# A one-core graph-attention layer: five more tiles add two products on VectorE, seven lists instead of eight beside the k|v rows, second half of the feed-forward weights asked later, x gathers pinned in their queue

## The chip, the cores and the metric

The kernel runs on 1 core of one Trainium2 chip. The metric is the device time of one execution in microseconds. A core has five engines with a queue each: TensorE (PE, its weight loads shown as PEld), VectorE (DVE), ScalarE (ACT), GpSimd (POOL) and SyncE (SP). Each works through its own queue in order. DMAs are started from the queues of SP, ACT and POOL; the indirect ones (gathers and scatters by row number) all come from POOL.

## The reference

One layer of masked attention over 4096 nodes with a feed-forward block, all in float32. `adj` holds about 17 edges in a row, so the work is sparse.

```python
hs = layer_norm(x, ln1_scale, ln1_bias); ht = layer_norm(h_target, ln1_scale, ln1_bias)
q = (ht @ Wq + bq).reshape(T, H, HD) / sqrt(HD)          # T = S = 4096, H = 8, HD = 64
k = (hs @ Wk + bk).reshape(S, H, HD)
v = (hs @ Wv + bv).reshape(S, H, HD)
logits = where(adj != 0, einsum('thd,shd->hts', q, k), -1e30)
probs = softmax(logits, axis=-1)
ctx = einsum('hts,shd->thd', probs, v).reshape(T, D)      # D = 512
ht = layer_norm(ht + ctx @ Wo + bo, ln2_scale, ln2_bias)
ff = gelu(ht @ W1) @ W2                                   # W1 512 x 2048, W2 2048 x 512
out = layernorm(x + ht + ff)
```

## The kernel before, in words

**First stage, to about 275 us.** Two things run side by side. `project` reads x, normalizes it and multiplies with Wk and Wv (L947); ScalarE copies the products (L949) and its queue writes rows of k|v, 1024 floats each, to a table `kvd` in DRAM (L953). `edges` turns a tile of 128 rows of `adj` into lists of neighbours: SP loads quarters of the rows (L714), ScalarE takes the sign and counts (L733), VectorE multiplies by column numbers (L740), finds the largest of segments (L742), and decodes and ranks them (L749 to L766). The 4096 target rows are handled in two parts of 16 tiles. `prepare` makes the lists of the first part and `sort(0)` orders its rows by degree with a scatter (L871). `fill` then makes `FILL = 8` list tiles of the second part while k|v rows are still being made. `RINGED` says how many tiles may load adj into free slots of the ring; later ones use two spare slots.

**Second stage, from about 277 us.** Sorted tiles of 128 targets are worked on in turn; the number of neighbour slots of a tile is its cap. In the order of work, tiles 0 to 15 are the first part with caps 11, 13, 14, 15, 15, 16, 17, 17, 18, 19, 19, 20, 22, 23, 24, 39, and tile 16 (12) begins the second part, with 38, 13, 24, 14, 23, 15 and so on after it. Tiles form groups: tile 0 alone, then pairs, and the last one alone. For a tile, `front` gathers the targets' rows, normalizes them (L1017, behind a small VectorE instruction L1013 that waits for the last k|v row) and makes the query (L1030, L1035). The slots go in segments of S = 3. `issue` gathers three rows of `kvd` per segment on POOL (L985) into a ring of 17 slots in the first part and 20 in the second; `request` keeps AHEAD = 4 segments asked for, five in the second part. VectorE multiplies k by the query (L1241) and sums (L1246), ScalarE takes the exponential (L1250, L1259). `by_scalar` multiplies the third slot's v on ScalarE, eight heads one by one (L1225); `values` multiplies the other two on VectorE (L1202). Each slot's product is then added up over the slots by TensorE as four transposes into PSUM (L1213, 128 x 128 each). In `values`, tiles from NA = 16 on first add slot 1 to slot 0 on VectorE (L1206), so slot 1 needs no transposes; from DENSE = 21 on every other segment also adds the third slot (L1209). `finish` scales by the softmax sum, multiplies by Wo (L1134) and normalizes.

**Feed-forward.** `feed` works one group at a time: `hidden` is W1 and gelu (L1346, L1349) and `output` is W2 (L1355). W1 and W2 come in four quarters of 2 MB each; two are loaded in the first stage, two by `weights` from the ACT queue (L586, L587) at the start of the second. Halfway through a group it gathers the group's x rows (L1373, recorded as L985 with tile xt), and `end` adds them, normalizes and scatters the result (L1323).

**Order.** `_weave` merges the streams by planned cost: every `yield` advances its stream's clock, and the stream that is furthest behind goes next. In the second stage attention and feed-forward take UNIT = 60 units for a pair of tiles; the lists of the second part start at WAIT = 100 units with 12 x 2.2 = 26.4 units a tile, and `sort(1)` follows them with 68 units. This gives the order of tracing. A scheduler then fills each engine's queue, mostly in that order, but an instruction whose inputs and buffers are free early may be put ahead. `with behind(ins)` (an `issue_after`) forbids that: what it holds stays in its engine's queue behind the instruction named. `issues` names the last gather that was traced. `newest` in `weights` names the last by_scalar product, so the ACT queue starts a weight load behind it.

Of the kernel before, what the change touches and what calls it, by code (L numbers as in the profile page):

```python
# [377 lines left out]
DEG, TGT, ROW, RST, E0 = 0, 1, 2, 3, 5  # L378
# [45 lines left out]
def _take(gen, n):  # L424

    for _ in range(n):
        cost = next(gen, StopIteration)
        if cost is StopIteration:
            return
        yield cost  # L430
# [13 lines left out]
def adj_resnorm_kernel(  # L444
# [56 lines left out]
    NA, NBT = len(CAPS_A), len(CAPS_B)  # L501
# [31 lines left out]
    with tc.tile_pool(name="keep", bufs=1) as keep:  # L533
# [13 lines left out]
        tags = keep.tile([P, NT, 2], I32, name="tags")  # L547
# [3 lines left out]
        with ExitStack() as late:  # L551
# [31 lines left out]
            def load_quarter(pool, q, engine=nc.sync):  # L583
                w1.append(pool.tile([P, KC, D], F32, name=f"w1_{q}"))
                w2.append(pool.tile([P, KC, D], F32, name=f"w2_{q}"))
                engine.dma_start(w1[q], W1[:, q * D:(q + 1) * D].rearrange("(c p) n -> p c n", p=P))  # L586
                engine.dma_start(w2[q], W2[q * D:(q + 1) * D, :].rearrange("(c p) n -> p c n", p=P))  # L587
# [115 lines left out]

            adjs = []
            DEEP = 8
            FILL = 8
            RINGED = NA + FILL - 1

            def quarter(i, h):
                if i < RINGED:  # L710
                    a = ring[:, (i * NQ + h) % DEEP, :].bitcast(I32)
                else:
                    a = turn_of("wide", wide)
                nc.sync.dma_start(a, adj[i * P:(i + 1) * P, h * QW:(h + 1) * QW])  # L714
                return a

            def behind(ins):
                return tc.issue_after(ins[-1]) if ins else nullcontext()

            def edges(i):  # L720
# [4 lines left out]
                for h in range(NQ):  # L725
# [9 lines left out]
                    while len(adjs) < min(max(n + 3, min(ahead, RINGED * NQ)), NT * NQ):  # L735
                        adjs.append(quarter(*divmod(len(adjs), NQ)))
                    yield 0.0 if i < NA else 0.7 if i < NA + FILL else 1.0
                    wd = sg.bitcast(U16)
# [6 lines left out]
                    if h % 2 and moms:  # L745
                        moments(moms.pop(0))
                    yield 1.8 if i < NA else 0.7 if i < NA + FILL else 1.0
                dec = dec_w
# [10 lines left out]
                for r in range(RE // 8):  # L759
                    top = rec[:, E0 + r * 8:E0 + (r + 1) * 8]  # L760
                    nc.vector.max(top, flat)
                    if r + 1 < RE // 8:
# [4 lines left out]
                                        op1=ALU.add, accum_out=cnt[:, i:i + 1])  # L767
                yield 2.4 if NA <= i < NA + FILL else 4.0

# [37 lines left out]
            def moments(i):  # L807

                while asked and len(asked) > NT - 4 - i:
                    ask(asked.pop(0))  # L810
                t = hrow(i)
                stats(ip, t, mvh[:, i, :], "n0")
# [169 lines left out]
            issues, logits = [], []  # L982

            def gather(dst, table, idx):
                issues[:] = [nc.gpsimd.indirect_dma_start(  # L985
                    out=dst, out_offset=None, in_=table[:, :],
                    in_offset=bass.IndirectOffsetOnAxis(ap=idx, axis=0)).ins]
# [71 lines left out]
            def request(k):  # L1059


                ahead = AHEAD + (1 if k >= first_b else 0)
                while issued[0] <= min(k + ahead, len(SG) - 1):
# [121 lines left out]
            def attention():  # L1185
# [10 lines left out]
                def values(i, j0, n, kv, p, cps, after):  # L1196

                    m = n - 1 if n == S else n  # L1200
                    v4 = kv[:, :m, D:].rearrange("p j (h d) -> p j h d", h=H)
                    nc.vector.tensor_tensor(v4, v4, p[:, j0:j0 + m, :].unsqueeze(3)  # L1202
                                            .to_broadcast([P, m, H, HD]), ALU.mult)
                    slots = list(range(n))
                    if m > 1 and i >= NA:
                        nc.vector.tensor_add(kv[:, 0, D:], kv[:, 0, D:], kv[:, 1, D:])  # L1206
                        slots.remove(1)
                        if n == S and i >= DENSE and j0 // S % 2:
                            nc.vector.tensor_add(kv[:, 0, D:], kv[:, 0, D:], kv[:, S - 1, D:])  # L1209
                            slots.remove(S - 1)  # L1210
                    for j in slots:
                        for c in range(KC):
                            nc.tensor.matmul(cps[:, c, :], kv[:, j, D + c * P:D + (c + 1) * P], ident,  # L1213
                                             is_transpose=True, start=j0 + j == 0 and c == 0,
                                             stop=j0 + n == TILES[i][1] and j == slots[-1],
                                             skip_group_check=True)
                    if after is not None:
                        tails.append(after)
# [112 lines left out]
            def feed(g):  # L1331
                while g not in h2Ts:
                    yield None
                group, h2T = GROUPS[g], h2Ts.pop(g)
                nt = len(group)
                w = nt * P
                fb = 4 // nt
                cost = UNIT * nt / 2 / (2 * FC // fb)
                xs = []
                po = [psf.tile([P, D], F32, name=f"po{j}", bufs=1) for j in range(nt)]  # L1340

                def hidden(f0):
                    pf = psf.tile([P, fb, w], F32, name="pf")
                    for k in range(fb):
                        for kc in range(KC):
                            nc.tensor.matmul(pf[:, k, :], w1[(f0 + k) // KC][:, kc, (f0 + k) % KC * P:((f0 + k) % KC + 1) * P],  # L1346
                                             h2T[:, kc, :w], start=kc == 0, stop=kc == KC - 1)
                    gt = sp.tile([P, fb, w], F32, name="gt")
                    nc.scalar.activation(gt, pf, AF.Gelu_apprx_tanh)  # L1349
                    return f0, gt  # L1350

                def output(f0, gt):
                    for j in range(nt):
                        for k in range(fb):
                            nc.tensor.matmul(po[j], gt[:, k, j * P:(j + 1) * P], w2[(f0 + k) // KC][:, (f0 + k) % KC, :],  # L1355
                                             start=False, stop=f0 + k == FC - 1, skip_group_check=True)

                def wind_up():
                    for e in list(ends):
                        if next(e, StopIteration) is StopIteration:  # L1360
                            ends.remove(e)

                last = hidden(0)
                wind_up()
                yield cost
                for f0 in range(fb, FC, fb):
                    now = hidden(f0)
                    wind_up()
                    yield cost
                    if f0 == FC // 2:  # L1370
                        for i in group:
                            xt = sp.tile([P, D], F32, name="xt")
                            gather(xt, x, tags[:, i, TGT:TGT + 1])  # L1373
                            xs.append(xt)
                    if f0 == fb:

                        for j in range(nt):
                            for kc in range(KC):
                                nc.tensor.matmul(po[j][:, kc * P:(kc + 1) * P],
                                                 h2T[:, kc, j * P:(j + 1) * P], ident,  # L1380
                                                 is_transpose=True, start=kc == 0, stop=False,
                                                 skip_group_check=True)
                    output(*last)
                    last = now
                    yield cost
                output(*last)
                yield cost
                ends.append(end(group, xs, po))
                if g + 1 == len(GROUPS):
                    while ends:  # L1390
                        wind_up()

                    nc.vector.scalar_tensor_tensor(flag, raised, xs[-1][0:1, 0:1], raised,  # L1393
                                                   op0=ALU.bypass, op1=ALU.max)
# [5 lines left out]

            WAIT = 100.0
            AHEAD = 4
            DENSE = 21
            UNIT = 60.0

# [41 lines left out]
            def fill():  # L1447
# [3 lines left out]
                yield 1.0  # L1451
                for cost in _take(ed, FILL * steps):
                    yield cost
# [9 lines left out]
            def weights():  # L1463


                for q, pool in enumerate(pools):
                    yield 10.0
                    with tc.issue_after(newest[-1]):
                        load_quarter(pool, q + 2, nc.scalar)

# [43 lines left out]
```

## Time and profile before

| | |
|---|---|
| median of 4 runs | 1802.0 us (1793.12 to 1813.67) |
| profiled execution | 1800.15 us, span 1798.4 us |
| mean granted TensorE clock | 0.971 |
| PE busy | 1665.9 us, 93% |
| DVE busy | 1412.2 us, 79% |
| ACT busy | 1223.3 us, 68% |
| POOL busy | 963.1 us, 54% |
| DMA | 461.01 MB, mean 256 GB/s |
| first and last L1206 | 1008.0 and 1656.2 us |
| first L1346, last L1355 | 348.1 and 1775.2 us |

Busy time is the time in which an engine had an instruction running; "idle before" in a list of groups or in brackets of a timeline is the time that the engine stood before that instruction, with what released it. A name such as kv<-kvd,rec is what the instruction writes and reads. The span is one execution's first to last instruction; the small rest up to the profiled execution's time is start and end.

### The profile page before, as it was taken

How to read it: one execution, taken by the hardware profiler on the slowest of the kernel's cores; microseconds unless marked ns; L12 is line 12 of the kernel's file. 1: busy time of each engine (PE TensorE's matmuls, PEld its weight loads, DVE VectorE, ACT ScalarE, POOL GpSimd, SP SyncE). 2: the span in 40 equal slices, each digit the busy share in tenths (PEclk: the TensorE clock that was granted, in tenths of full speed). 3: DMA queues.
4: the chain of work that ended last, by engine and by line, in shares of the span. 5: the costliest groups of instructions: out<-in, count | busy, mean ns of one | idle time of the engine just before them, and what ended most of it. 6: DMA issues, size and time to landing. Idle time of an engine off the chain costs nothing. (4 is left out here: it accounts for less than half of the span.)

```text
span 1798.4 us, 22591 instructions
## 1 busy us (share of the span) xinstructions
PE 1665.9 (93%) x6918; PEld 1082.8 (60%) x6918; DVE 1412.2 (79%) x2432; ACT 1223.3 (68%) x3121; POOL 963.1 (54%) x818
## 2 busy tenths in 40 slices
PE   7999994797999999998998999989999999999995
PEld 3444442665666666666676666655666666666663
DVE  6887787988888779776878999798889888988100
ACT  5876673668677877665767787677878677776210
POOL 1000147745545556787667787867475676671100
PEclk9999997898999999999999999999999999999997
DMA  9999989968878777679778898778686777782000
GB/s 354 381 393 356 349 276 371 340 237 293 268 240 295 234 264 242 226 244 310 251 247 306 284 300 279 237 271 266 205 290 225 268 252 238 238 280 92 24 1 26
DMA packets 142060, 461.01 MB, mean 256 GB/s; under 512 B 18549, under 2 KB 23497, under 8 KB 141929
## 3 DMA queue, kind: packets, MB, share of 16 engines
q0 software_dynamic: 96144, 342.27, 56.2%
q1 hardware_dynamic: 37968, 94.12, 14.8%
q10 hardware_dynamic: 7816, 23.08, 3.3%
q8 instruction: 57, 0.93, 0.2%
q14 instruction: 75, 0.61, 0.1%
HBM read 430.61 MB, written 28.79 MB: 255 GB/s over the span
## 5 line engine op out<-in xcount | busy, mean ns | idle before, releaser
L985 POOL DMA_INDIRECT kv<-kvd,rec x603 | 745.9, 1237 | 329.0 <-PE cps L1213 140.9
L1355 PE MATMUL po<-w,gt 128*128 128x512 f32 x1024 | 465.1, 597 | 5.3 <-ACT gt L1349 5.3
L1346 PE MATMUL pf<-h2T,w 128*128 128x256 f32 (+1 forms) x2176 | 464.4, 367 | 0.3 <-ACT h2T L1165 0.3
L1346 PEld LDWEIGHTS pf<-h2T,w 128*128 128x128 f32 x2176 | 388.0, 190 | 63.6 <-issue 19.6
L1241 DVE TENSOR_TENSOR kv<-kv,tq 128x1536 f32<-128x1536 f32 (+2 forms) x211 | 351.4, 1674 | 77.1 <-DMA kv<-kvd,rec 61.1
L1225 ACT ACTIVATE kv<-kv,pa 128x64 f32<-128x64 f32 x1520 | 391.9, 336 | 4.6
L1246 DVE TENSOR_REDUCE lg<-kv 128x24 f32<-128x1536 f32 (+2 forms) x211 | 350.3, 1666 | 0.7
L1355 PEld LDWEIGHTS po<-w,gt 128*128 128x128 f32 x1024 | 188.8, 192 | 200.9 <-issue 193.6
L1213 PEld LDWEIGHTS cps<-ident,kv 128*128 128x128 f32 x1896 | 225.2, 144 | 98.4 <-issue 42.7
L1213 PE MATMUL cps<-ident,kv 128*128 128x128 f32 x1896 | 250.2, 279 | 33.8 <-DVE kv L1202 26.9
L1202 DVE TENSOR_TENSOR kv<-kv,p 128x1024 f32<-128x1024 f32 (+1 forms) x211 | 250.5, 1191 | 13.9 <-ACT p L1250 13.9
L687 POOL TENSOR_TENSOR n_rs<-n_ve,mhalf 128x2 f32<-128x2 f32 (+2 forms) x51 | 49.2, 964 | 341.6 <-DVE n_ve L680 166.4
L733 ACT ACTIVATE kv<-kv 128x1024 uint8<-128x1024 int32 x128 | 134.4, 1052 | 56.1 <-DMA kv<-in_adj_dram 18.4
L1349 ACT ACTIVATE gt<-pf 128x512 f32<-128x512 f32 x128 | 76.4, 597 | 93.7 <-PE pf L1346 92.6
L1030 PE MATMUL t<-wq,tq 128*128 128x512 f32 x256 | 124.0, 630 | 16.6 <-ACT tq L1024 16.6
L1349 ACT ACT_TABLE_LOAD x104 | 133.4, 1283 | 1.7
L947 PE MATMUL pq<-wv,h2T 128*128 128x512 f32 x256 | 117.1, 601 | 7.1 <-ACT kv L949 4.3
L947 PE MATMUL pq<-wk,h2T 128*128 128x512 f32 x256 | 119.0, 608 | 0.7 <-DMA wk<-in_L_gnn_Wk_dram 0.7
L1134 PE MATMUL t<-wo,rb 128*128 128x512 f32 x256 | 115.5, 593 | 0.0
L1250 ACT ACTIVATE p<-lg 128x24 f32<-128x24 f32 (+2 forms) x179 | 39.0, 218 | 104.0 <-DVE lg L1246 103.0
L742 DVE MAX8 cand<-kv 128x8 uint16<-128x171 uint16 (+1 forms) x384 | 108.1, 324 | 1.2
L1030 PEld LDWEIGHTS t<-wq,tq 128*128 128x128 f32 x256 | 50.2, 202 | 75.5 <-issue 48.4
(163 smaller groups left out, 1561.9 us busy)
## 6 DMA issues: line engine op xcount, KB each, us to landing
kv<-in_adj_dram SPq DMA_DIRECT2D x128, 512.0 KB, 6.8
kvd<-tq ACTq DMA_DIRECT2D x23, 512.0 KB, 6.8
kv<-kvd,rec POOLq DMA_INDIRECT x603, 5.8
kv<-in_L_gnn_h_target_dram SPq DMA_DIRECT2D x32, 256.0 KB, 6.3
kv<-in_x_dram SPq DMA_DIRECT2D x15, 512.0 KB, 7.9
kvd<-kv ACTq DMA_DIRECT2D x9, 512.0 KB, 9.5
w<-in_L_gnn_W_dram SPq DMA_DIRECT2D x4, 1024.0 KB, 7.8
w<-in_L_gnn_W_dram ACTq DMA_DIRECT2D x4, 1024.0 KB, 15.3
```

What stands on the lines that cost most here:

```text
L733: nc.scalar.activation(sg, a, AF.Sign, accum_out=dpart[:, i, h:h + 1])
L947: nc.tensor.matmul(pkv, hT[:, kc, j * P:(j + 1) * P], w[:, kc, :], start=kc == 0, stop=kc == KC - 1)
L985: issues[:] = [nc.gpsimd.indirect_dma_start(out=dst, out_offset=None, in_=table[:, :], in_offset=bass.IndirectOffsetOnAxis(ap=idx, axis=0) ...
L1030: nc.tensor.matmul(pq, hT[:, kc, :], wq[:, kc, :], start=kc == 0, stop=kc == KC - 1)
L1202: nc.vector.tensor_tensor(v4, v4, p[:, j0:j0 + m, :].unsqueeze(3) .to_broadcast([P, m, H, HD]), ALU.mult)
L1213: nc.tensor.matmul(cps[:, c, :], kv[:, j, D + c * P:D + (c + 1) * P], ident, is_transpose=True, start=j0 + j == 0 and c == 0, stop=j0 + n ...
L1225: newest[:] = [nc.scalar.mul(v, v, pa[:, hd:hd + 1]).ins]
L1241: nc.vector.tensor_tensor(kv[:, :n, :D], kv[:, :n, :D], tq[:, :D].unsqueeze(1).to_broadcast([P, n, D]), ALU.mult)
L1246: logits[:] = [nc.vector.tensor_reduce(lg[:, :n, :], kv[:, :n, :D].rearrange("p j (h d) -> p j h d", h=H), AX.X, ALU.add).ins]
L1346: nc.tensor.matmul(pf[:, k, :], w1[(f0 + k) // KC][:, kc, (f0 + k) % KC * P:((f0 + k) % KC + 1) * P], h2T[:, kc, :w], start=kc == 0, stop= ...
L1349: nc.scalar.activation(gt, pf, AF.Gelu_apprx_tanh)
L1355: nc.tensor.matmul(po[j], gt[:, k, j * P:(j + 1) * P], w2[(f0 + k) // KC][:, (f0 + k) % KC, :], start=False, stop=f0 + k == FC - 1, skip_g ...
```

## The change

Four edits. In `values` the limit from which two products are added on VectorE goes from NA = 16 to ADDS = 11, so tiles 11 to 15 add too. FILL goes from 8 to 7, so one list tile moves from the first stage to the lists beside the attention (and RINGED from 23 to 22). The gather of x rows in `feed` is put behind the last gather traced before it. `weights` waits 26 planned units instead of 10 before the third quarter; the fourth then follows at 36 instead of 20.

```diff
-            FILL = 8
+            FILL = 7
             RINGED = NA + FILL - 1
...
-                    if m > 1 and i >= NA:
+                    if m > 1 and i >= ADDS:
                         nc.vector.tensor_add(kv[:, 0, D:], kv[:, 0, D:], kv[:, 1, D:])
                         slots.remove(1)
...
                             xt = sp.tile([P, D], F32, name="xt")
-                            gather(xt, x, tags[:, i, TGT:TGT + 1])
+                            with behind(issues):
+                                gather(xt, x, tags[:, i, TGT:TGT + 1])
                             xs.append(xt)
...
             AHEAD = 4
+            ADDS = 11
             DENSE = 21
...
                 for q, pool in enumerate(pools):
-                    yield 10.0
+                    yield 26.0 if q == 0 else 10.0
                     with tc.issue_after(newest[-1]):
                         load_quarter(pool, q + 2, nc.scalar)
```

## The prediction

> **What bounds the kernel now.** I read the page's busy shares first, then a table of stretches (the first attention tile, the stage of the last five tiles of the first part, a group after it), then the waits of that stage, and last the timeline of the change of stages.
>
> ```profile
> PE 1665.9 (93%) x6918; PEld 1082.8 (60%) x6918; DVE 1412.2 (79%) x2432; ACT 1223.3 (68%) x3121; POOL 963.1 (54%) x818
> ```
>
> TensorE is busy 93% of the span, VectorE 79%. By stretches (columns: stretch in us, its length, then busy time of PE, PEld, DVE, ACT, POOL, the granted clock, DMA share, GB/s):
>
> ```profile
> 288.20:313.10 24.90, 7.14 (x38) 5.28 (x36) 18.15 (x13) 7.34 (x31) 19.86 (x17) 0.76 1.03 403
> 348.10:730.40 382.30, 358.58 (x1668) 247.98 (x1667) 311.96 (x530) 280.55 (x718) 216.60 (x186) 0.97 0.75 258
> 730.40:832.10 101.70, 98.05 (x461) 68.31 (x460) 73.20 (x78) 67.17 (x183) 80.56 (x73) 1.00 0.79 257
> 832.10:927.10 95.00, 89.61 (x434) 63.57 (x433) 80.01 (x86) 68.93 (x199) 58.26 (x51) 1.00 0.78 261
> 927.10:1002.80 75.70, 70.55 (x330) 49.88 (x329) 63.88 (x55) 56.32 (x162) 54.26 (x46) 0.95 0.86 293
> 1028.90:1121.60 92.70, 90.54 (x410) 61.18 (x409) 92.08 (x95) 71.81 (x210) 73.78 (x55) 1.00 0.87 288
> ```
>
> The limits are found from the first L1246 of each tile. 288 to 313 is tile 0: no engine is full, the DMA is. 730 to 832 is tiles 11 and 12 (20 and 22 slots), 832 to 927 tiles 13 and 14 (23 and 24), 927 to 1003 tile 15 (39): these five get the new add. There TensorE is idle 14.2 of 272.4 us and VectorE 55.3. So TensorE sets the pace, with VectorE not far behind. 1029 to 1122 is the group of 38 and 13 slots, which adds already: VectorE is busy 92.08 of 92.7 us (0.993), so it can be loaded to the brim in this loop. After 1672 only feed-forward matmuls are left, 108 us that no edit touches.
>
> **The adds.** A segment is three slots; ScalarE takes the third, VectorE the other two, so each segment with at least two slots left gets one add L1206 and loses the four transposes L1213 of slot 1. The caps 20, 22, 23, 24, 39 make 7 + 7 + 8 + 8 + 13 = 43 adds and 172 transposes fewer.
>
> ```profile
> L1213 PE MATMUL cps<-ident,kv 128*128 128x128 f32 x1896 | 250.2, 279 | 33.8 <-DVE kv L1202 26.9 <-DVE kv L1206 6.7
> L1206 DVE TENSOR_TENSOR kv<-kv 128x512 f32<-128x512 f32 x101 | 68.5, 681 | 0.3
> ```
>
> On VectorE: 43 x 0.681 = 29.3 us more. On TensorE: 250.2/1896 = 0.132 us each by busy time, but the timeline has twelve that start at 380.64 with the next work at 381.95, so 0.109 us from start to start; I take the second, 172 x 0.109 = 18.8 us less (22.7 by the first). What of it reaches the end, group by group:
> - Tiles 11, 12: TensorE 98.05 - 14 x 0.436 = 91.9 busy, VectorE 73.2 + 9.5 = 82.7. TensorE still leads; all 6.1 us come off.
> - Tiles 13, 14: VectorE 80.0 + 16 x 0.681 = 90.9 overtakes TensorE (89.6 - 7.0 = 82.6). The floor is 90.9/0.993 = 91.5 against 95.0: 3.5 us.
> - Tile 15: VectorE 63.9 + 8.9 = 72.8, floor 73.3 against 75.7: 2.4 us.
>
> Sum 12 us. Bounds: 0 if VectorE's waits stay as they are; 18.8 if VectorE's run-ahead lets TensorE keep all.
>
> What can spoil the floor is that VectorE's idle time here is waits, which do not fill by themselves (waits of VectorE from 730 to 1003: total us, times, longest):
>
> ```profile
> DVE kv L1241 <- DMA kv<-kvd,rec: 22.7, 13, 6.4
> DVE tq L1035 <- PE t L1030: 13.4, 2, 8.0
> ```
>
> The first (L1241 behind gathers) shrinks when VectorE comes later to the data, the second when TensorE comes sooner. I therefore let the adds fill them. POOL's gathers are touched as well. In the timeline after 430 us, the 193 kv gathers whose first 0.94 us overlaps no VectorE instruction with two SBUF tensors took 0.95 us on POOL, the 334 that overlap one took 1.41. That is 334 x 0.46 = 154 us on 650 us of such VectorE work, 0.24 per us; the adds make 29.3 x 0.24 = 7 us, and POOL is idle 80 us in this stage. I put it at nothing; if POOL's cover were gone it is 7 us.
>
> The Trainium skill has a rule that speaks against this edit: its page GPSIMD Engine Reference (section 8, Key points) says that GpSimd shares its SBUF interfaces with VectorE and contends with instructions that have two SBUF inputs, which the add is. The rule gives no size; read as the whole 29.3 us lost to POOL it would still fit in the 80 us of POOL's idle time, and the rows' 7 us fits better, so both leave the sum as it is.
>
> **Seven list tiles instead of eight.** One list tile is on VectorE 4 x (0.41 + 3 x 0.324) + 3.2 (the decode and the three rounds of L761/L763) = 8.7 us, on ScalarE 4 x (1.052 + 0.191) = 5.0 us, and 2 MB of adj. It leaves the end of the first stage and joins the lists beside the attention, where it ends in the planner's units at 100 + 9 x 26.4 = 338 instead of 311, and sort(1) with its sixteen POOL scatters L871 at 406 instead of 379, that is in tiles 10 to 13 and not 10 to 12; prefetch of the second part's first records is traced at about 407 and used two tiles later. In its new place TensorE leads (358.6 of 382.3 us busy from 348 to 730) and VectorE has 70 us idle: cost 2 us, bounds 0 and 8.7. POOL's scatters (1.0 us each) are the same number, moved past gathers in a stage with POOL 80 us idle.
>
> **The change of stages** holds the gain of this edit, of the pin and of the later weights (timeline: start, us, engine, line):
>
> ```profile
> 270.85 0.33 ACTq L953 DMA_DIRECT2D kvd<-kv  x1
> 273.73 1.23 POOL L985 DMA_INDIRECT xt<-in_x_dram,tags  x1 [11.98 <-DVE tags L1016]
> 275.09 1.06 ACT L733 ACTIVATE kv<-kv 128x1024 uint8<-128x1024 int32 x1 [1.44 <-DMA kv<-in_adj_dram]
> 276.15 1.50 ACT L1017 ACTIVATE tq<-tq,rec 128x512 f32<-128x512 f32 x2
> 277.06 0.94 POOL L985 DMA_INDIRECT kv<-kvd,rec  x1 [0.85 <-DMA kv<-in_adj_dram]
> 286.43 1.76 DVE L1241 TENSOR_TENSOR kv<-kv,tq 128x1536 f32<-128x1536 f32 x1
> 300.08 0.52 ACTq L587 DMA_DIRECT2D w<-in_L_gnn_W_dram  x1
> 305.32 1.76 DVE L1241 TENSOR_TENSOR kv<-kv,tq 128x1536 f32<-128x1536 f32 x1 [2.24 <-DMA kv<-kvd,rec]
> 311.47 1.76 DVE L1241 TENSOR_TENSOR kv<-kv,tq 128x1536 f32<-128x1536 f32 x1 [4.39 <-DMA kv<-kvd,rec]
> ```
>
> The eighth list tile's signs (L733 at 267.3, 268.4, 272.5, 275.1) stand ahead of the first query's L1017, and its VectorE work ahead of L1013. Without it L1017 runs some 4.6 us sooner. But the first gather needs the last kvd row (written from 270.85), and then 1.24 us per issue and 5.8 us to land: data at 279.56 + 5.8 = 285.4, so only 1.0 of the 4.6 counts, plus up to 3.4 us if signs hold the last k|v copies less (PE waited 3.39 us at 258.8 for L949). I take 2, bounds 0 and 4.6. The two x gathers at 273.73 and 275.28 are the only ones ahead of the attention; pinned behind the last gather traced they leave POOL's queue, 2 x 1.24 = 2.5 us, but the kvd row is the cover: 0, within the same bounds. Later x gathers already stand behind gathers that were traced earlier: 0.
>
> **The weights.** The four 1 MB loads (ACT queue, 290.4 to 300.5) take 4 MB / 403 GB/s = 10.4 us out of a DMA that is full, while gathers come every 1.24 us. VectorE then waits 2.24 + 4.39 = 6.6 us before 313, with TensorE (11.4 us at 304.7 to 316.1) behind it. After the change the first pair goes out at 26 units instead of 10, after the third segment's ScalarE products (about 300 us), the second at 36 instead of 20, in tile 1 (about 315). By then gathers have run ahead: a segment costs 3 x 1.24 = 3.7 us of DMA and 4.6 us of VectorE. A pair delays them 5.2 us, under the four segments (18 us) that are asked ahead. The weights are used from 369 on (third L1346 block), so they have 40 us. Gain 6.6 us; bounds 6.6 and 0 (the hole only moves to tiles 1 and 2, where VectorE is never idle).
>
> **Sum** on the profiled execution, 1800.15 us (span 1798.4 and 1.75 around it): - 12.1 (adds) - 2 (start) - 6.6 (weights) + 2 (list) = -18.7, so 1781.5, say **1782 us**. The profiled time stands 1.85 us under the median 1802.0, inside the runs' 1793 to 1814. About 1% (18 us) is what a measurement of this kernel can tell from no change, so the forecast lies just past that line, below 1784. Its own range, 1773 to 1791, comes from half of each term's bounds.
>
> **Rivals.**
> - The adds turn to nothing (chance 0.16): VectorE's waits for gathers and L1030 stay, and TensorE's freed time becomes waits on L1206. For it: groups after 1122 already show PE waiting for L1206 (6.7 us in all); against: the group at 0.993. 1781.5 + 12.1 = 1794.
> - The weights' hole only moves (0.14): the ring of 17 slots is short, POOL waits for slots already at 317 and 322. Against: the run-ahead above. 1781.5 + 6.6 = 1788.
> - More is won (0.11): from 409.1 to 420.4 TensorE stands 11.29 us behind L1017, which waits for a tq gather that POOL issued late at 411.13. If the new order of POOL's queue issues it in time, 1781.5 - 11.3 = 1770.
> - Slower (0.14): VectorE is on the path all along. In each segment the product, the sum, the new add and the next product are one queue, with four segments ahead and 17 ring slots, not five and 20 as after 1029. Then 29.3 + 8.7 = 38 us are added and 8.6 won at the stages: 1800.15 + 29.4 = 1830. It decides from the point where more than 8.6 of the 38 us are not hidden. Against it: 55.3 us of VectorE idle in the five tiles and 14.2 of TensorE.
>
> **How the numbers follow.** Forecast 0.45, of which 0.34 under 1784; with "more is won" 0.11 that makes faster 0.45. Within 1%: 0.11 + 0.16 + 0.14 + 0.02 of the slow rival = 0.43. Slower 0.12. The range, 1763 to 1812, takes in the first three rivals and the bounds (adds 18.8, start 4.6: 1772; the won stall below that), and leaves out most of the slow one.
>
> **What would show it.** First L1241 near 284 to 285 and no wait on kvd gathers in tile 0; tile 1 from about 305; first L1346 near 340, not 348. The weights' DMAs after 297. 144 L1206 instead of 101, 1724 L1213 instead of 1896. Tiles 11 to 15 in about 260 us instead of 272, VectorE over 90% busy from 832 on. The lists' last L740 some 25 to 40 us later than 683.7. I am wrong if these five tiles take 270 us or more, if tile 1 starts no earlier than 311, or if PE waits for L1206 by more than 15 us before tile 16.

## The result, and the profile after

The changed kernel takes 1797.8 us (median), the kernel before beside it 1798.9 us: ratio 0.9992, 95% interval 0.9982 to 1.0001. No difference can be measured, where 1782 us was forecast. The profiled execution took 1803.2 us (span 1801.4, granted clock 0.962), before 1800.15 us (span 1798.4, 0.971).

The page's busy shares of the changed kernel:

```profile
PE 1661.5 (92%) x6746; PEld 1074.8 (60%) x6746; DVE 1432.7 (80%) x2475; ACT 1230.6 (68%) x3125; POOL 1008.4 (56%) x818
```

The instruction counts are those of the change: 172 matmuls fewer, 43 VectorE instructions more. VectorE is 20.5 us busier, yet TensorE only 4.4 us less busy, though 172 x 0.109 = 18.8 us of work had gone (the last section shows where the rest went), and POOL is 45 us busier with the same 818 instructions. Groups of instructions (busy, mean ns | idle before and what ended it):

```profile
L1213 PE MATMUL cps<-ident,kv 128*128 128x128 f32 x1724 | 240.1, 286 | 66.0 <-DVE kv L1206 39.8 <-DVE kv L1202 25.9
L1206 DVE TENSOR_TENSOR kv<-kv 128x512 f32<-128x512 f32 x144 | 97.8, 680 | 0.3
```

An add is as long as the forecast said, 0.680 us. But TensorE stands 39.8 us for adds (6.7 us before), and a transpose is a little longer, 286 ns against 279.

Stretches of the changed kernel (length, then busy time of PE, PEld, DVE, ACT, POOL, the granted clock, DMA share, GB/s): tile 0, tile 1, tiles 11 and 12, 13 and 14, 15.

```profile
291.80:308.70 16.90, 7.85 (x36) 6.65 (x36) 16.15 (x13) 7.24 (x31) 13.55 (x12) 0.63 0.97 343
308.70:339.00 30.30, 17.31 (x77) 13.63 (x78) 23.49 (x25) 12.77 (x48) 20.88 (x18) 0.59 1.04 404
725.90:822.00 96.10, 90.01 (x386) 61.11 (x385) 85.70 (x102) 70.12 (x184) 71.59 (x59) 0.96 0.76 245
822.00:917.80 95.80, 83.92 (x349) 56.37 (x349) 85.25 (x89) 70.08 (x198) 77.99 (x60) 0.91 0.80 266
917.80:997.70 79.90, 70.40 (x310) 48.17 (x309) 69.58 (x70) 57.62 (x164) 61.33 (x48) 0.98 0.84 286
```

Tiles 11 to 15 take 96.1 + 95.8 + 79.9 = 271.8 us, before 272.4. Pairs of tiles move by some microseconds either way (101.7, 95.0 and 75.7 before), and the sum does not. VectorE is busy 89% and 87% of the last two stretches, not over 90%. Tiles 0 and 1 take 47.2 us, before 46.2: tile 0 won 8.0 us and tile 1 lost 9.0. The change of stages, in the timeline:

```profile
270.05 1.06 ACT L733 ACTIVATE kv<-kv 128x1024 uint8<-128x1024 int32 x1 [5.00 <-DMA kv<-in_adj_dram]
273.92 0.33 ACTq L953 DMA_DIRECT2D kvd<-kv  x1
276.74 1.52 ACT L1017 ACTIVATE tq<-tq,rec 128x512 f32<-128x512 f32 x2 [2.85 <-DVE rec L1013]
280.95 0.97 POOL L985 DMA_INDIRECT kv<-kvd,rec  x1 [18.27 <-DMA rest_d<-gid]
289.54 1.76 DVE L1241 TENSOR_TENSOR kv<-kv,tq 128x1536 f32<-128x1536 f32 x1 [1.89 <-DMA kv<-kvd,rec]
303.92 0.39 ACTq L586 DMA_DIRECT2D w<-in_L_gnn_W_dram  x1
313.15 1.76 DVE L1241 TENSOR_TENSOR kv<-kv,tq 128x1536 f32<-128x1536 f32 x1 [1.31 <-DMA kv<-kvd,rec]
315.30 0.38 ACTq L586 DMA_DIRECT2D w<-in_L_gnn_W_dram  x1
325.24 1.76 DVE L1241 TENSOR_TENSOR kv<-kv,tq 128x1536 f32<-128x1536 f32 x1 [2.48 <-DMA kv<-kvd,rec]
```

A sign (L733) of the seventh list waits 5.00 us for its adj ahead of the last k|v copies, so the last kvd row goes out at 273.92 (before 270.85), and the first gather and the first L1241 are 3 to 4 us later, not 1 to 2 earlier. One trace does not make this the edit's doing: in the fourteen kernels traced for this document that keep eight lists and free x gathers, the first L1241 starts between 283.6 and 291.7 us, in the five with seven lists between 285.1 and 289.5. The weights went out from 303.9, and VectorE now waits for gathers in tile 1 instead of tile 0. One thing did go: the stall of 11.29 us at 409 us is not there, and tile 4 takes 26.4 us, before 33.9 (tile 3 took 1.8 us more). A few us in one tile can be chance: in the six traces that change nothing ahead of tile 11, tile 3 takes 41.6 to 47.6 us, tile 4 32.7 to 34.2.

### The profile page after: what moved, and what is told of

Its sections match the earlier page's. It is cut to its first block, busy times and chain, and to the rows that moved or that the text cites. A ratio compares the mean times of both kernels' runs of the same rounds, so it can differ in the third digit from the quotient of the medians.

```text
span 1801.4 us, 22277 instructions
## 1 busy us (share of the span) xinstructions
PE 1661.5 (92%) x6746; PEld 1074.8 (60%) x6746; DVE 1432.7 (80%) x2475; ACT 1230.6 (68%) x3125; POOL 1008.4 (56%) x818
## 5 line engine op out<-in xcount | busy, mean ns | idle before, releaser
L985 POOL DMA_INDIRECT kv<-kvd,rec x603 | 777.9, 1290 | 356.8 <-PE cps L1213 140.1
L1355 PE MATMUL po<-w,gt 128*128 128x512 f32 x1024 | 470.3, 601 | 2.8 <-ACT gt L1349 2.7
L1346 PE MATMUL pf<-h2T,w 128*128 128x256 f32 (+1 forms) x2176 | 467.1, 368 | 0.6 <-ACT h2T L1165 0.6
L1346 PEld LDWEIGHTS pf<-h2T,w 128*128 128x128 f32 x2176 | 388.6, 191 | 65.2 <-issue 20.1
L1241 DVE TENSOR_TENSOR kv<-kv,tq 128x1536 f32<-128x1536 f32 (+2 forms) x211 | 351.7, 1674 | 47.2 <-DMA kv<-kvd,rec 29.6
L1246 DVE TENSOR_REDUCE lg<-kv 128x24 f32<-128x1536 f32 (+2 forms) x211 | 350.7, 1665 | 0.5
L1213 PE MATMUL cps<-ident,kv 128*128 128x128 f32 x1724 | 240.1, 286 | 66.0 <-DVE kv L1206 39.8
L1213 PEld LDWEIGHTS cps<-ident,kv 128*128 128x128 f32 x1724 | 212.5, 148 | 136.0 <-DVE kv L1206 53.3
L687 POOL TENSOR_TENSOR n_rs<-n_ve,mhalf 128x2 f32<-128x2 f32 (+2 forms) x51 | 50.5, 989 | 330.5 <-DVE n_ve L680 159.5
L733 ACT ACTIVATE kv<-kv 128x1024 uint8<-128x1024 int32 x128 | 134.4, 1052 | 55.6 <-DMA kv<-in_adj_dram 22.0
L1206 DVE TENSOR_TENSOR kv<-kv 128x512 f32<-128x512 f32 x144 | 97.8, 680 | 0.3
```

Of the source, the lines that this page charges most:

```text
L733: nc.scalar.activation(sg, a, AF.Sign, accum_out=dpart[:, i, h:h + 1])
L985: issues[:] = [nc.gpsimd.indirect_dma_start(out=dst, out_offset=None, in_=table[:, :], in_offset=bass.IndirectOffsetOnAxis(ap=idx, axis=0) ...
L1241: nc.vector.tensor_tensor(kv[:, :n, :D], kv[:, :n, :D], tq[:, :D].unsqueeze(1).to_broadcast([P, n, D]), ALU.mult)
L1246: logits[:] = [nc.vector.tensor_reduce(lg[:, :n, :], kv[:, :n, :D].rearrange("p j (h d) -> p j h d", h=H), AX.X, ALU.add).ins]
```

## Experiments

All are timed in five rounds against the kernel before; each ratio is to that kernel, with its 95% interval, and a percentage is of its time (18 us are 1%).

### Each edit by itself, and each left out

```diff
# adds alone
-  if m > 1 and i >= NA:
+  if m > 1 and i >= 11:
# seven lists alone
-  FILL = 8
+  FILL = 7
# later weights alone
-  yield 10.0
+  yield 26.0 if q == 0 else 10.0
# pin alone
-  gather(xt, x, tags[:, i, TGT:TGT + 1])
+  with behind(issues):
+      gather(xt, x, tags[:, i, TGT:TGT + 1])
```

Adds alone:

> Kernel before with the adds in tiles 11 to 15 alone. Theory A (the adds pay nothing: VectorE's 29 us come to stand where TensorE's 19 us were): 0.997 to 1.003 of before, tiles 11 to 15 in 268 to 276 us, TensorE waiting for L1206 by 15 us or more in them. Theory B (the adds pay their 12 us, another edit takes it back): 0.992 to 0.995, the five tiles in about 260 us.

Seven lists alone:

> Kernel before with seven list tiles beside the k|v rows instead of eight, alone. Theory A (the last list tile's signs stand ahead of the last k|v copies whichever tile it is, so the first stage ends no sooner): last k|v row written at 270 us or later, time 0.998 to 1.004. Theory B (this edit is the one that costs): 1.004 to 1.008, with VectorE fuller beside the lists and the later scatters holding up gathers.

Later weights alone:

> Kernel before with the third and fourth weight quarter asked at 26 and 36 units, alone. Theory A (the hole only moves from tile 0 into tile 1): tile 0 is 5 to 8 us shorter and tile 1 as much longer, tile 2 begins within 3 us of 334, time 0.998 to 1.002. Theory B (the later request pays what was forecast): tile 2 begins near 328, time 0.996.

Pin alone:

> Kernel before with the x gathers behind the last gather traced, alone. Both theories: the two early x gathers at 274 us leave the start of the attention, first kv gather within 1.5 us of 277, time 0.998 to 1.002. If the x gathers were what held up POOL (29 us of waits for the result's scatter before, 7 after), the time falls to 0.996 or less.

Measured: adds 1.0031 (1.0004 to 1.0058), the only one that differs from 1, and it is slower; seven lists 1.0001 (0.9975 to 1.0028); later weights 0.9981 (0.9951 to 1.0010), with tiles 0 and 1 at 45.6 us and the stall at 409 gone; pin 1.0015 (0.9986 to 1.0043). So the adds do not win the 12 us of the forecast: they cost 5.6 us (0.7 to 10.4). The four sum to +0.28%, the whole change is at -0.08%; with some 0.28% either way on each of the four, that gap alone shows nothing. The changed kernel with one part left out:

> The changed kernel without its adds: seven lists, weights asked at 26 units, x gathers pinned, limit of the adds back at 16. Theory A (the adds cost some 5 us and the other three win as much back, mainly by the stall after 409 us that is gone): 0.27% to 0.4% faster than before, 1792 to 1795 us where before is 1799, and the time from the first L1246 of tile 11 to that of tile 19 stays at 391 us (399 in the changed kernel). Theory B (the other three are nothing, and the adds together with them are nothing too): ratio 0.999 to 1.001, and the adds would be innocent here.

> The changed kernel, but x gathers not pinned. The adds cost 0.31% on top of the kernel before and win 0.25% on top of the other three edits. If the pin is what turns them (x gathers out of GpSimd's queue ahead of the root and of the kv gathers), ratio to before 1.002 or above here. If the later weights are, 0.999 here. If nothing single does, 0.9985 to 1.0015.

> The changed kernel, but the weights asked at 10 units as before. If the later weights turn the adds' loss into a gain (the stall after 409 us was gone with them), ratio to before 1.002 or above. If the pin does, 0.999. If nothing single does, 0.9985 to 1.0015.

Measured: without the adds 1.0017 (0.9998 to 1.0037), without the pin 1.0036 (1.0014 to 1.0058), without the later weights 1.0006 (0.9983 to 1.0029). My reading that three edits win back what the adds lose is wrong: without the adds the other three are not faster than before. Within the change the adds are worth 0.9992 - 1.0017 = -0.25% and the pin 0.9992 - 1.0036 = -0.44% (some 0.2% either way), while each alone gave no gain. The two edits as a pair, without the rest, were not run. The pin's place can be seen. GpSimd's timeline before, then VectorE's behind it:

```profile
626.68 1.81 POOL L985 DMA_INDIRECT xt<-in_x_dram,tags  x1 [3.84 <-DMA out_dram<-xt,tags]
638.79 1.12 POOL L985 DMA_INDIRECT xt<-in_x_dram,tags  x1 [3.90 <-DMA out_dram<-xt,tags]
650.03 1.76 DVE L1241 TENSOR_TENSOR kv<-kv,tq 128x1536 f32<-128x1536 f32 x1 [4.83 <-DMA kv<-kvd,rec]
```

Two x gathers wait for a scatter that still reads their buffer, with the kv gathers queued behind them, and VectorE stands 4.83 us for such a gather. In the changed kernel the pair comes later and waits for nothing:

```profile
651.05 0.95 POOL L985 DMA_INDIRECT xt<-in_x_dram,tags  x1 [0.30 <-issue]
652.30 2.47 POOL L985 DMA_INDIRECT xt<-in_x_dram,tags  x1 [0.30 <-issue]
```

Tile 9 takes 47.1 us with the pin (47.6 with the pin alone) and 54.5 before (54.0 in the change without it). Where the pin stood alone, those 7 us were lost again: tiles 17 and 18 took 99.2 us, before 92.7.

### What the adds cost, and to whom

Three kernels on the one before: slot 1's transposes left out in tiles 11 to 15 without any add (its v is missing from the result); the adds with all transposes kept (slot 1 is counted twice); the add over half of the columns with no transposes of slot 1 (half of its v is missing).

```diff
# no transposes
+  if m > 1 and 11 <= i < NA:
+      slots.remove(1)
# adds and transposes
+  if m > 1 and 11 <= i < NA:
+      nc.vector.tensor_add(kv[:, 0, D:], kv[:, 0, D:], kv[:, 1, D:])
# half adds
+  if m > 1 and 11 <= i < NA:
+      nc.vector.tensor_add(kv[:, 0, D:D + D // 2], kv[:, 0, D:D + D // 2],
+                           kv[:, 1, D:D + D // 2])
+      slots.remove(1)
```

> Kernel before, with the transposes of slot 1 left out in tiles 11 to 15 and no add put in their place (slot 1 is missing from the sum there). Theory A (TensorE's 19 us are worth having, VectorE's 29 us eat them): 12 to 19 us come off, ratio 0.989 to 0.994, the five tiles in 253 to 260 us. Theory B (TensorE's time in these tiles is not on the path at all, what is taken off becomes waiting): 0.997 to 1.000.

> Kernel before, with the add in tiles 11 to 15 put in and all transposes kept (slot 1 is counted twice there). Theory A (each add is partly on the path): 12 to 25 us more, ratio 1.007 to 1.014. Theory B (VectorE's 55 us of idle time take the adds, and TensorE's saving is what is worth nothing): 0.999 to 1.003.

> Tiles 11 to 15 with slot 1's transposes left out and the add done over 256 of the 512 columns (the v part of the result lacks the other half). No add at all gave -11.5 us, the whole add +5.6. Theory A (VectorE's added time is paid in proportion: 17 us for 29.3 us): the half add takes about 0.40 us each, 17 us in all, and the kernel stands at -11.5 + 10 = -2 us, ratio 0.999. Rival (a threshold: there is room for some VectorE work that costs nothing, and only the last part is paid): -8 us or more, ratio 0.9955 or below.

Measured: 0.9936 (0.9913 to 0.9958), 1.0038 (1.0020 to 1.0055) and 0.9978 (0.9960 to 0.9996). TensorE's 18.8 us are worth 11.5 us (7.6 to 15.7) when VectorE pays nothing, so its path does lead, but not by all of them. The half adds take 43 x 0.42 = 18 us and the whole ones 29.3, but VectorE's busy time from tile 11 to 18 grows by only 13.5 and 24.3 us against the kernel without any, because an instruction here starts before the one ahead of it has ended (seen below at 967.80). These three kernels stand at -11.5, -4.0 and +5.6 us: VectorE's added busy time is paid at 17.1/24.3, some 0.7 us per us, and in part from the first (7.5 for 13.5; each difference has 5 to 6 us either way). With the transposes kept the adds cost 6.8 us, so in their presence TensorE's saving is worth only about 1 us (the two intervals leave some 5 us either way). The forecast's best place was tiles 11 and 12:

```diff
-  if m > 1 and i >= NA:
+  if m > 1 and (i >= NA or i in (11, 12)):
```

> Adds in tiles 11 and 12 alone, where the forecast had all 6.1 us coming off because VectorE is busy 73 of 102 us there. Forecast's theory: -6 us, ratio 0.9966. Theory A (VectorE's stream is the path, and about half of its added work reaches the end whatever TensorE is spared): 14 x 0.68 = 9.5 us of adds give +2 to +5 us, less some us of the transposes: ratio 0.999 to 1.002. Theory C (the harm is in tile 15 and the 38-slot tile alone, where VectorE is fullest): ratio 0.997 or below here.

Measured: 0.9997 (0.9979 to 1.0015). The 6.1 us that were to come off here, where VectorE was busy 73 of 102 us, do not come.

What VectorE does with its idle time is read from one stretch in all kernels, from the first L1246 of tile 11 to that of tile 19, columns as above. Before; adds alone:

```profile
730.40:1121.60 391.20, 374.84 (x1752) 261.84 (x1751) 333.12 (x337) 288.27 (x815) 286.29 (x238) 0.99 0.82 274
```

```profile
730.20:1136.90 406.70, 369.02 (x1584) 250.58 (x1584) 356.59 (x380) 292.08 (x818) 305.60 (x236) 0.95 0.78 262
```

VectorE works 23.5 us more in it and is idle 406.7 - 356.6 = 50.1 us, before 58.1: the adds filled 8 us of its waits and made the stretch 15.5 us longer. The 43 more instructions are the adds, and VectorE's other work in the stretch is the same, line by line; so the 29.3 us of the forecast were 23.5 of busy time. Behind the stretch 7.3 us are won back (669.4 us to the end, before 676.8), with 2648 matmuls left instead of 2652; how is not shown. Without adds and with them on top of the other three edits:

```profile
722.50:1125.50 403.00, 375.66 (x1736) 260.96 (x1735) 339.53 (x351) 287.88 (x814) 295.27 (x238) 0.97 0.78 266
```

```profile
725.90:1124.70 398.80, 364.41 (x1566) 246.43 (x1565) 360.85 (x393) 294.78 (x819) 304.22 (x236) 0.96 0.80 267
```

Here VectorE was idle 63.5 us without the adds and is idle 38.0 with them: 25 us filled, and the stretch shorter by 4.2, no more than single tiles differ from trace to trace. The three edits bring the work to tile 11 some 5 to 8 us earlier (725.9 and 722.5, before 730.4) and without the adds lose that in this stretch as waits; there the adds find room. This agrees with the change of sign, but no run shows why the waits fill in the one order of work and not in the other.

### Which wait keeps VectorE from filling

The first suspect was the ring: 17 slots and four segments ahead in the first part, 20 and five in the second.

```diff
-  if place[-1] + n > RING[i >= NA]:
+  if place[-1] + n > RING[i >= 13]:
-  first_b = next(k for k, (i, _, _) in enumerate(SG) if i >= NA)
+  first_b = next(k for k, (i, _, _) in enumerate(SG) if i >= 13)
```

> Kernel before, with the ring of 20 slots and five segments asked ahead from tile 13 on instead of tile 16, no adds. Theory C (the ring is what limits tiles 13 to 15 once adds are there, not without): 0.996 to 1.002, waits of L1241 for gathers in tiles 13 to 15 down from 15 us. If gathers limit these tiles in any case: 0.995 or less.

> Kernel before with the adds in tiles 11 to 15 and the ring of 20 slots and five segments ahead from tile 13 on. Theory C (an add holds slot 1 until L1206 and slot 0 until TensorE comes after it, so the ring of 17 runs dry; with 20 slots it does not): tiles 13 to 15 fall from 178 us with the adds alone to 165 or less, ratio 0.993 to 0.997. Theory A (VectorE is the bound, the ring has nothing to do with it): tiles 13 to 15 stay at 173 us or more, ratio 1.000 to 1.004.

Measured: the ring alone 0.9946 (0.9924 to 0.9968), with the adds 1.0046 (1.0020 to 1.0072). The longer ring is worth 9.7 us without the adds and nothing with them; so beside it the adds cost 1.0046 - 0.9946 = 1.0%, 18 us (some 6 either way). Where the ring alone wins is not shown: VectorE's waits for gathers in tiles 11 to 15 are 22.9 us with it, 22.7 before. In the trace with ring and adds VectorE waits 8.8 us for gathers there (20.6 with the adds alone), but 19.0 us for L687, the reciprocal root that GpSimd computes for a norm (6.7 with the adds alone). That wait can be followed in the changed kernel, in tile 15:

```profile
957.16 0.15 DVE L680 TENSOR_SCALAR n_ve<-mv 128x2 f32<-128x2 f32 x1
958.81 0.98 POOL L985 DMA_INDIRECT xt<-in_x_dram,tags  x1 [2.43 <-DMA out_dram<-xt,tags]
960.09 3.10 POOL L985 DMA_INDIRECT tq<-in_L_gnn_h_target_dram,rec  x1 [0.30 <-issue]
966.97 0.72 POOL L687 TENSOR_TENSOR n_rs<-n_ve,mhalf 128x2 f32<-128x2 f32 x1
967.73 0.16 DVE L692 SCALAR_TENSOR_TENSOR n_nm<-mv,n_rs 128x2 f32<-128x2 f32 x1 [5.36 <-POOL n_rs L687]
967.80 0.69 DVE L1206 TENSOR_TENSOR kv<-kv 128x512 f32<-128x512 f32 x1
968.40 1.75 DVE L1246 TENSOR_REDUCE lg<-kv 128x24 f32<-128x1536 f32 x1
968.54 1.85 PE L1213 MATMUL cps<-ident,kv 128*128 128x128 f32 x8 [4.50 <-DVE kv L1206]
```

The root's input is there at 957.3. Its 0.72 us start at 966.97, behind gathers. VectorE stands 5.36 us for it with the add next in its queue, and TensorE stands for the add. So the root was taken out of GpSimd's queue: a VectorE copy of the variance stands in its place in both norms of a group, and the outputs are scaled by the variance instead of its reciprocal root.

```diff
-  rs = power(sp, mv[:, :nh, :], nh, "n2", ve)
+  rs = sp.tile([P, nh], F32, name="n2_rs")
+  nc.vector.tensor_copy(rs, ve)
...
-  rs = power(sp, None, nt, "n3", ve)
+  rs = sp.tile([P, nt], F32, name="n3_rs")
+  nc.vector.tensor_copy(rs, ve)
```

> The kernel before, in which the reciprocal root of the two norms at a group's end (GpSimd's L687 as L1148 and L1313 call it) is left out: a VectorE copy of the variance stands in its place, so no norm waits in GpSimd's queue. VectorE stood 30 us for it between 300 and 1700 us before. Theory P (GpSimd's queue decides only where VectorE leads): before, TensorE leads, so little: -0.1% to -0.4%, 1792 to 1797 us where before is 1799. Rival (the root is on the path already in the kernel before): -1% or more.

> The same with the adds in tiles 11 to 15. Alone the adds cost 5.6 us. Theory P (what spoils them is that each add stands in VectorE's queue behind a norm that waits 5 to 10 us for the root in GpSimd's queue, with TensorE waiting for the add): without the root the adds gain, 4 to 12 us under the kernel without root and without adds, ratio to before 0.990 to 0.995. Rival (VectorE's stream is long in itself, the root only one of its waits): the adds cost the same 3 to 6 us against the kernel without root, ratio 0.999 to 1.002.

With the ring as well:

> Adds in tiles 11 to 15, ring of 20 slots and five segments asked ahead from tile 13, root left out of the two norms (a VectorE copy in its place). It takes away both of VectorE's outside waits in tiles 13 to 15: those for gathers (short in adds_ring, 9 us) and those for the root (absent in adds_no_root). Theory W (each of the two waits takes the other's place, so that taking one away is not enough): ratio to before 0.984 or below, 7 us or more under the adds without root (0.9908). Theory V (VectorE's stream itself is too long in groups 8 and 9, whatever it waits for): 0.988 to 0.993.

Measured: without the root 0.9842 (0.9812 to 0.9871), with the adds 0.9908 (0.9881 to 0.9935), with adds and ring 0.9918 (0.9895 to 0.9940). The root is on the path already in the kernel before: without it 28 us go, about as much as VectorE stood for it (29.9 us between 300 and 1700 us). Whether that standing went or the shorter chain to the feed-forward is not shown by this run. TensorE then multiplies other values; its granted clock is 0.975 against 0.971, so up to 0.4% could come from there. The theory that it spoils the adds is wrong: without it the adds cost 0.9908 - 0.9842 = 0.66%, 12 us (some 7 either way), no less than with it. With both waits attacked the stretch still looks like this:

```profile
717.50:1123.80 406.30, 371.06 (x1601) 251.53 (x1600) 360.79 (x395) 297.42 (x829) 310.91 (x234) 0.96 0.80 267
```

VectorE is idle 45.5 us of 406.3, 11%. With the adds and only the root gone it is 11% as well, with the adds and only the ring longer 13%. In tiles 11 to 15 it still waits 14.2 us for gathers, and 16.2 us ahead of L1241 for something the profile does not name. So neither the root nor the short ring by itself is what holds the adds back; that no outside wait does is not shown.

### A version that beats both

The ring from tile 13 alone already does (1791.4 us, 0.9946). Two more were tried: with the later weights, and with VectorE's L692 traced two segments later behind the root.

```diff
   rs = power(sp, mv[:, :nh, :], nh, "n2", ve)
   yield
+  yield
+  yield
   nm = negmean(sp, mv[:, :nh, :], rs, nh, "n2")
```

> A version meant to beat both: the kernel before with the later weights and with the ring of 20 slots and five segments asked ahead from tile 13 instead of 16. The two alone gave -0.19% and -0.54%. If they act in different places (the stall after 409 us, and tiles 13 to 15), they add up: ratio 0.9927, 1786 us where before is 1799. If the weights' gain is lost later as the hole of the first tiles was, 0.9946.

> A version meant to beat both, with the whole reference computed: the kernel before with the ring of 20 slots from tile 13, and with VectorE's L692 traced two segments later behind the root (two more yields ahead of L1150), so that VectorE does not stand for GpSimd's queue. If the 28 us that the missing root won were VectorE's standing (30 us) alone, most of it comes back here: ratio 0.982 to 0.988. If they were the shorter chain to h2T and the feed-forward matmuls, nothing: 0.994 to 0.997, or worse, since the chain gets longer by some 10 us a group.

Measured: 0.9954 (0.9932 to 0.9976) for the weights, no more than the ring alone; 0.9874 (0.9847 to 0.9901) for the later L692, 1780.5 us, the fastest kernel here that computes all of the reference. Its time is what I expected, but my reason for it is not in the trace. The waits before, and of this version, over the whole run:

```profile
DVE n_nm L692 <- POOL n_rs L687: 39.6, 26, 11.0
```

```profile
DVE n_nm L692 <- POOL n_rs L687: 41.2, 27, 8.0
```

VectorE still stands as long for the root. Against the trace of the ring alone, tiles 3 to 6 take 154.0 us instead of 169.2, and later tiles give some back. TensorE's long wait there for L1017 (the stall at 409) is 4.1 us instead of 10.6, which is less than half of it; which part of the new order does the rest stays open.

## Why the prediction was wrong, by its own steps

- **The counts** were right: 144 L1206, 1724 L1213, 0.68 us an add. But 43 x 0.681 = 29.3 us took an add's length for what it adds to VectorE's busy time, which grew by 23.5 us with the adds alone. The 108 us of feed-forward after 1672 are 104 us of TensorE, and a few of its matmuls are others.
- **The adds (-12.1 us)** are the step that failed. "The floor is 90.9/0.993" took one group, 38 and 13 slots at 0.993, as what VectorE can be filled to, and "I therefore let the adds fill them" turned its waits into room. Alone the adds cost 5.6 us (1.0031), and nothing measurable comes off in tiles 11 and 12 (0.9997, -0.21% to +0.15%), where all 6.1 us (0.34%) were to. VectorE's share of the stretch of tiles 11 to 18 was 0.85 before, 0.88 with the adds alone and 0.90 in the changed kernel. Even the group of 38 and 13 slots is no longer full: 101.7 us with VectorE busy 95.05. Two of the text's three marks for being wrong came: five tiles over 270 us (271.8), and PE waiting for L1206 by 25.7 us in tiles 11 to 15, over the 15 named. The third, tile 1 no earlier than 311, did not (308.7).
- **TensorE's saving** was sized right as work (18.8 us) and too large as time: 11.5 us without any add, about 1 us with them. The forecast counted it at the clock of before; TensorE's work at a lower clock took 14.0 us of it back in the changed kernel (last section).
- **The slow rival** (VectorE on the path all along) came nearest, with too large a price: it charged all 38 us of added work; measured, some 0.7 us per us of VectorE's busy time, with TensorE's saving against it.
- **The start (-2 us)** cannot be seen: the first L1241 is 3.1 us later in this trace and 1.3 us earlier than before in the changed kernel without its adds (285.1), within what it differs between kernels with the same first stage. The first L1346 came at 354.9, not near 340. **The list tile (+2)** cannot be seen: seven lists alone 1.0001.
- **The weights (-6.6 us)**: the rival "the hole only moves", at 0.14, is what the trace shows, tile 0 -8.0 and tile 1 +9.0 us. What they won was the stall at 409, which stood in "more is won"; alone that is 0.9981, not distinguishable from 1.
- **The pin (0)** was mis-sized. "Later x gathers already stand behind gathers that were traced earlier: 0" left out that GpSimd waits for a buffer at 12 of the 32 x gathers, 29.2 us in all in the waits of before, with kv gathers behind it. Afterwards it is 6.8 us, and within the change the pin is worth 0.44%, alone nothing that can be measured.
- **GpSimd (7 us, put at nothing)**: in the stretch of tiles 11 to 18 a kv gather took 1.22 us before and 1.31 with the adds alone, 194 x 0.09 = 18 us. Not all of this is the adds': with slot 1's transposes gone and no add it is already 1.26, and in the changed kernel it is 1.29 with the adds and 1.26 without, about the 7 us of the forecast. Gathers beside no VectorE instruction with two SBUF inputs stay at 0.95 us, before and with the adds alone; those beside one go from 1.33 to 1.42. The Trainium skill's page GPSIMD Engine Reference (section 8, Key points) says that GpSimd contends with VectorE instructions that have two SBUF inputs. These rows agree in direction; whether the longer gathers are on the path no run shows.

The measured -1 us cannot be told from nothing. The adds lose in the old order of work; in the new one adds and pin each show a small gain beside the other edits, and what turns the sign stays open.

## What to carry to other kernels

Do not take an engine's idle time for room. Here 58 us of VectorE's stood in the stretch, and 23.5 us of work filled 8 us of it and made the stretch 15.5 us longer. A likely reason, argued and not tested, is that VectorE, TensorE, GpSimd's queue and the ring wait for each other in a circle, so that a wait moves with the work. Do not price a busy-time floor by the fullest group in the trace, and test moved work by itself and beside the other edits before summing: the adds cost 0.31% alone, 1.0% on the longer ring, 0.66% without the root, and won 0.25% beside the other three edits. A short instruction that an in-order queue puts behind DMA issues (0.7 us of root in GpSimd's) can be worth more than the edit under study: 28 us went with it, in a kernel that scales by other values.

## What the runs showed that was not expected

**The granted clock falls with TensorE's waits.** In the stretch of tiles 11 to 18 it is 0.99 before and 0.95 with the adds alone; over the whole run 0.971 before, 0.962 with the adds alone, 0.975 without the root and 0.963 without the root but with the adds. In the timeline above, the eight transposes right after the 4.50 us wait took 1.85 us; eight shortly before it took 1.04:

```profile
959.55 1.04 PE L1213 MATMUL cps<-ident,kv 128*128 128x128 f32 x8
```

The stretches around that wait (columns as above, the clock third from the end) show the clock halved right behind it:

```profile
963.00:968.50 5.50, 1.05 (x5) 0.57 (x3) 0.77 (x3) 0.58 (x1) 4.37 (x6) 1.00 0.66 190
968.70:972.10 3.40, 3.40 (x17) 3.40 (x17) 2.79 (x3) 3.37 (x8) 2.79 (x3) 0.50 0.86 264
```

In these traces the clock is only ever 1.0 or 0.5. Each of the twelve spells at half clock between 300 and 1200 us of the changed kernel begins during, or within 1.3 us after, a wait of TensorE of 2.4 us or more; one wait of 2.87 us outside them is followed by none. So a wait of TensorE can cost more than its own length. Over the whole run 104.6 us are at half clock before, 136.3 in the changed kernel and 135.6 with the adds alone. As an estimate, half of the time that TensorE is busy in them would not have been needed at the full clock: 28.5, 42.5 and 36.6 us. Without it TensorE would have been busy 1637.4 us before and 1619.0 in the changed kernel, 18.4 us less, which is the forecast's 18.8; 14.0 of them went into the lower clock (8.1 with the adds alone). How much of this is on the path no run separates from VectorE's added time.

**A gather lengthens even where no VectorE work is added**: 1.22 us before and 1.26 with only the transposes gone, 1.31 with the adds alone.
